# A two-layer attention and mixture-of-experts kernel: rank sums moved to TensorE, a softmax sum left out, one batch's residual adds moved to VectorE, and a denser queue of follow-up work

## The chip, the cores and the metric

The kernel runs on one core of one Trainium2 chip. Its time is the device time of one execution in microseconds, the median of several runs. A core has five instruction engines that matter here, each working through its own queue in order: TensorE (PE, with its weight loads shown apart as PEld), VectorE (DVE), ScalarE (ACT), GpSimd (POOL) and SyncE (SP), which here only starts transfers and reads registers. Data types are fp32 throughout.

## The reference

Two layers run on `x` of shape 8 x 512 x 256 (8 batches of 512 tokens, 256 channels). Each layer is an attention and a routed feed-forward, both behind a layer norm with a per-batch scale and shift, and both added back to `x` through a per-batch gate. Cut to what matters for the change:

```python
# layer 0 feed-forward, 4 experts, F = 1024
probs = softmax(xf @ router_w + router_b)
top_p, top_i = top_k(probs, 2)
top_p = top_p / sum(top_p)
out = sum over the two experts of top_p * (silu(xf @ w1[e]) * (xf @ w3[e])) @ w2[e]

# layer 1 attention; scores are 16 x 16 blocks, heads of width HD = 4
qkvw = x @ w_qkvw
o = softmax(q @ k.T * HD ** -0.5) @ v
x = x + ga * ((o * w) @ w_out)

# layer 1 feed-forward, 8 experts
route = sigmoid(x @ Wr + br)
out = max(route) * gelu(x @ W1[e]) @ W2[e]      # e = argmax(route)
```

The gates of layer 0's two experts are divided by their own sum. A common factor on both, such as the softmax's denominator, cancels there. Layer 0's attention is a running sum over tokens (a causal one), so it needs a scan over the 512 tokens of a batch for every head.

## The kernel before

**Chunks.** A feed-forward is not computed for all experts and all tokens. Tokens are sorted by expert into slots in DRAM (`hs`), and TensorE works on tiles of 128 rows of one expert. Six `Moe` objects hold six chunks: `m0` and `m1` are layer 0, four batches each (35 tiles each, two experts per token); `m2` and `m3` are layer 1 for the even batches, `m4` and `m5` for the odd ones (two batches each; 13 tiles each are run in the main order).

**A route.** `route(i)` is a generator that puts batch `i` of a chunk into slots, in four parts that a `yield` separates. Part one normalises `x` (`stats`, `normed`; bn_stats is L180). Part two transposes (`ptr`, L506), computes the logits (`pl`, L511), and transposes the modulated rows back (`prow`, L519) into `ht`, the rows to be scattered. Part three adds the bias (`z`, L527), takes the layer's function, and finds the chosen expert with `first_max` (L455 to L460), which leaves a one-hot `ch` for each token and choice. For layer 0, `now` is the sum of both choices (L546). Still in part three, VectorE writes `pre` (L560 to L566): `pre[:, t]` holds how often each expert was chosen by the tokens of earlier groups of 128, started from the running count of earlier batches. The fourth part, after a `yield`, ranks each token among those of its expert: `pk` is `tri` (a triangle of ones) times `now` (L569), plus `ones` times `pre` (L570). After another `yield`, VectorE makes slot numbers of the ranks (`rank`, `at`, `pos`, L573 to L582), and GpSimd starts one scatter per group and choice (`indirect_dma_start`, L586). `table()` then multiplies `ones` by the running count (`pn`, L603), and makes with some twenty small VectorE operations the table from which SP reads each tile's expert and first row.

**Layer 0's attention.** `attend0(b)` runs scans on VectorE (L411) and products on TensorE (`pv` L405, `poa` L422). Its results go to `residual` (L233, L234): VectorE multiplies by the gate, GpSimd adds to `x`. Batches 0 to 3 run before `m0`, woven with the routes of `m0`: batch `b`'s attention goes beside the route of batch `b - 1`, and the route of batch 3 (`HB - 1`, `HB` is 4) stands alone, followed by `m0.table()`. Batches 4 to 7 and the routes of `m1` go beside the tiles of `m0`.

**The order of tiles and steps.** `Line.run(m, steps, n, at, follow)` writes the tiles of a chunk in program order. A tile is a first half of the up-products (`up`, L760), the second half of the tile before's down-products (`down`, L775), the load of the next tile's rows (`xs`, transposed at L733), and then its own second halves. Twice in each tile, `n(j) / 2` steps are taken from the generator `steps`. So `n` is the number of steps beside a tile, and `at` names work for certain tiles (negative keys count from the end; `until(m4, steps)` takes steps until `m4` has its table). There is no planner: each engine does its instructions in the order in which the program wrote them.

**Layer 1's attention.** `attend(half, ...)` is such a generator: `half` 0 is batches 0 to 3 beside `m1`, `half` 1 is batches 4 to 7 beside `m2`, `m3` and `m4`. It goes in 16 units (4 output chunks of 4 units each). `step(u, v, w)` writes one unit's VectorE operations (a product, four sums, a maximum, reductions; L1011 to L1065), and every operation is followed by a `yield`; a full unit is 16 of them. GpSimd has part of the products (`far`, L996, and `farv`, L1031). `project` writes the projections (`pqk`, L978). When all four units of a chunk are done, `finish(i, after)` is put at the end of a list `behind`. `finish` transposes `o` (`pot`, L1078), copies it with ScalarE (`owT`, L1083), multiplies by the output weights (`pao`, L953), adds to `x` on VectorE (L957), and then runs what `then` holds for this chunk: for `half` 1 the routes of `m4` (chunks 0 and 1), with `m4`'s table, and of `m5` (chunks 2 and 3), with `m5`'s table. `beside(main)` passes on the steps of a unit and, after every third one, takes one step from the first generator in `behind`. Whatever is left of `behind` is taken after the last unit.

After a chunk is computed, `fetch_results` loads its rows back (`yl`, GpSimd's queue, L810), and `combine` multiplies by the gate and adds to `x` (L825 and L829).

```python
a2 = chain(attend(0, owA), m2.route(0), m2.route(1), ready(m2))
line.run(m1, a2, lambda j: 11.5 if j > 2 else 0, {...}, m2)
steps = attend(1, {}, {0: [m4.route(0)], 1: [m4.route(1), ready(m4)], 2: ..., 3: ...})
line.run(m2, steps, lambda j: 11 if j > 5 else 0, {..., 11: [until(m3, after)]}, m3, J=m2.J - 2)
line.run(m3, steps, lambda j: 11, {-3: [until(m4, steps)]}, m4, J=m3.J - 2)
line.run(m4, steps, lambda j: 6, {-3: [until(m5, steps)]}, m5, J=m4.J - 2)
drain(steps)
line.run(m5, iter(()), lambda j: 0, {...}, J=m5.J - 2)
```

Of the kernel before, what the change touches and what calls it, by code (L numbers as in the profile page):

```python
# [9 lines left out]
F32 = mybir.dt.float32  # L10
# [4 lines left out]
P = 128  # L15
# [13 lines left out]
def kernel(  # L29
# [200 lines left out]
    def residual(po, gate, b, t, name):  # L230

        tmp = wk.tile([P, D], F32, tag="tmp", name=name, bufs=2)
        nc.vector.tensor_mul(tmp, po, gate)  # L233
        nc.gpsimd.tensor_tensor(x[b][:, t, :], x[b][:, t, :], tmp, ALU.add)  # L234

# [226 lines left out]
    class Moe:  # L462
# [19 lines left out]
        def route(self, i):  # L482
# [51 lines left out]
            if l == 0:  # L534
                s = wk.tile([P, NT], F32, tag="rs", name=f"s{b}")
                nc.vector.tensor_reduce(s, z, AX.X, ALU.max)
                nc.vector.tensor_tensor(z, z, bcast(s, E), ALU.subtract)
                nc.scalar.activation(z, z, AF.Exp)
                nc.vector.tensor_reduce(s, z, AX.X, ALU.add)
                nc.vector.reciprocal(s, s)  # L540
                nc.vector.tensor_mul(z, z, bcast(s, E))
                first_max(z, E, m[0], ch[0], f"a{b}")
# [15 lines left out]

            pre = fp.tile([P, NT + 1, E], F32, tag=f"pre{E}", name=f"pre{bm}", bufs=3)
            if i == 0:  # L560
                nc.vector.memset(pre[:, 0], 0.0)
            else:
                nc.vector.tensor_copy(pre[:, 0], self.run_)
            for t in range(NT):
                nc.vector.tensor_add(pre[:, t + 1], pre[:, t], now[:, t])
            self.run_ = pre[:, NT]  # L566
            yield
            pk = ps_m([P, NT, E], f"pk{bm}")
            nc.tensor.matmul(pk, tri, now, start=True, stop=False)  # L569
            nc.tensor.matmul(pk, ones, pre[:, :NT], start=False, stop=True)  # L570
            yield
# [387 lines left out]
    def attend(half, owTs, then={}):  # L959
# [138 lines left out]
        def beside(main):  # L1098
            for n, _ in enumerate(main):
                yield  # L1100
                if n % 3 == 2 and behind:
                    if next(behind[0], behind) is behind:
                        behind.pop(0)
# [71 lines left out]
    def late():  # L1175
# [10 lines left out]
    after = late()  # L1186
    line.run(m2, steps, lambda j: 11 if j > 5 else 0, {
        0: [fetch_all(m1)],
# [7 lines left out]
    }, m3, J=m2.J - 2)  # L1196
    line.run(m3, steps, lambda j: 11, {-3: [until(m4, steps)]}, m4, J=m3.J - 2)
    line.run(m4, steps, lambda j: 6, {-3: [until(m5, steps)]}, m5, J=m4.J - 2)
    drain(steps)
# [75 lines left out]
```

## Time and profile before

Three runs took 1987.05, 1991.45 and 2002.29 us. The profiled execution took 2008.8 us by the same measure, 0.9% over their median; in it 2007.1 us lie between the first and the last instruction.

| | |
|---|---|
| median of the runs | 1991.45 us |
| profiled execution, its span | 2008.8 us, 2007.1 us |
| TensorE busy | 1764.3 us, 88% |
| VectorE busy | 1259.4 us, 63% |
| ScalarE, GpSimd busy | 717.4 us, 589.8 us |
| transfers | 488.6 MB, 243 GB/s |
| mean granted TensorE clock | 0.932 |

The span falls into stages, by the first and last products of each chunk in the trace: first attention and routing to about 330 us; `m0` to 880; `m1` to 1380; `m2` to 1567; `m3` to 1749; `m4` to 1888; `m5` to 1987; then the last results. The shares of busy time are means over stages of different kinds, and say little by themselves.

The costliest lines show what fills TensorE:

```profile
L760 PE MATMUL p<-xT,w 128*128 128x128 f32 x6144 | 770.2, 282 | 29.3 <-DMA w<-in_W_dram 17.9
L775 PE MATMUL po<-w_d,g 128*128 128x256 f32 x1952 | 483.3, 388 | 33.1 <-DVE g L767 22.8
L234 POOL TENSOR_TENSOR x<-x,ra 128x256 f32<-128x256 f32 x32 | 24.8, 780 | 141.2 <-DVE ra L233 141.0
L565 DVE TENSOR_TENSOR pre<-pre,ch 128x8 f32<-128x8 f32 x32 | 6.4, 202 | 0.4
L570 PE MATMUL pk<-pre,ones 128*128 128x16 f32 (+1 forms) x32 | 7.2, 307 | 5.2 <-DVE pre L565 5.2
```

Each row has the line, the engine and operation, the tile written and the tiles read, the shape, the count, then busy us and mean ns of one, then the idle time of the engine just before these instructions and what ended most of it. The up- and down-products are 71% of TensorE's busy time. The rows that the change touches are small: 24.8 us on GpSimd for all residual adds, 6.4 us on VectorE for layer 1's sums of `pre`, 7.2 us on TensorE for their products.

### The profile page before, as it was taken

To read this page: it belongs to the slowest core of one execution; us is meant where nothing else is said; L and a number is where in the kernel's file an instruction comes from. 1 tells how busy PE (TensorE), PEld (TensorE's weight loads), DVE (VectorE), ACT (ScalarE), POOL (GpSimd) and SP (SyncE) were. 2 spreads that over 40 slices of the span, in tenths; PEclk is the share of its full clock that TensorE was granted. 3 is DMA by queue.
4 is the path that set the end of the run, shared out by engine and by line. 5 is a ranking of instruction groups with operands and counts; after the bars stand their busy time and mean duration, and the time that the engine had idled before them with its cause. 6 is when DMAs were issued, how large, how long until landed. Compare 5 with 4: busy or idle time off the path is not lost.

```text
span 2007.1 us, 32461 instructions
## 1 busy us (share of the span) xinstructions
PE 1764.3 (88%) x11336; PEld 1541.1 (77%) x11336; DVE 1259.4 (63%) x2228; ACT 717.4 (36%) x1372; POOL 589.8 (29%) x564
## 2 busy tenths in 40 slices
PE   6786866989989989989999999998969989799895
PEld 3354436878878878879899898897868878788785
DVE  5786875443443532225999999722599999986200
ACT  5053112321312212216444435532545546355221
POOL 1033132121121121222444533123245464542110
PEclk8797887999999999989999999999989999899898
DMA  7877768899899997886786777888744655579795
GB/s 231 214 221 198 173 170 277 234 310 279 255 289 280 295 312 237 289 312 231 229 277 229 230 236 230 269 284 295 260 138 135 216 176 185 187 246 344 248 348 167
DMA packets 328536, 488.60 MB, mean 243 GB/s; under 512 B 24017, under 2 KB 184049, under 8 KB 327729
## 3 DMA queue, kind: packets, MB, share of 16 engines
q1 hardware_dynamic: 313840, 445.17, 71.9%
q0 software_dynamic: 14528, 41.31, 5.5%
q8 instruction: 92, 1.51, 0.3%
q14 instruction: 76, 0.61, 0.1%
HBM read 446.40 MB, written 45.27 MB: 245 GB/s over the span
## 4 chain that ended last, share of the span: by engine, by line
PE 53%; DVE 24%; DMA 9%; issue 7%; ACT 4%; POOL 2%; SPq 1%; another core or an unknown queue 1%; DVEq 0%; ACTq 0%; POOLq 0%
PE p L760 23%; PE po L775 13%; PE poa L422 3%; PE pv L405 3%; DVE u L411 3%; DMA w<-in_W_dram 3%; PE pqk L978 3%; DVE s L1019 2%; DVE o L1043 2%; DVE g L767 2%; DMA w<-in_w_dram 1%; DVE o L1060 1%; PE pl L511 1%; DVE u L414 1%; DMA ratio<-rows 1%
## 5 line engine op out<-in xcount | busy, mean ns | idle before, releaser
L760 PE MATMUL p<-xT,w 128*128 128x128 f32 x6144 | 770.2, 282 | 29.3 <-DMA w<-in_W_dram 17.9
L760 PEld LDWEIGHTS p<-xT,w 128*128 128x128 f32 x6144 | 750.3, 198 | 43.9 <-issue 18.0
L775 PE MATMUL po<-w_d,g 128*128 128x256 f32 x1952 | 483.3, 388 | 33.1 <-DVE g L767 22.8
L775 PEld LDWEIGHTS po<-w_d,g 128*128 128x128 f32 x1952 | 357.8, 194 | 87.5 <-DVE g L767 27.9
L790 POOL DMA_INDIRECT ys<-y,to x122 | 151.4, 1241 | 676.8 <-ACT xT L735 413.1
L765 ACT ACTIVATE g<-p 128x512 f32<-128x512 f32 x244 | 145.7, 597 | 482.4 <-PE p L760 411.9
L767 DVE TENSOR_TENSOR g<-g,p 128x512 f32<-128x512 f32 x140 | 95.6, 683 | 293.8 <-PE p L760 238.7
L411 DVE TENSOR_TENSOR_SCAN u<-ratio,pv 128x512 f32<-128x512 f32 x128 | 149.6, 1204 | 54.7 <-PE pv L405 35.5
L405 PE MATMUL pv<-hT,wv_sb 128*128 128x512 f32 x256 | 138.8, 664 | 34.4 <-DVE u L411 27.4
L996 POOL TENSOR_TENSOR far<-q 128x1024 f32<-128x1024 f32 x64 | 133.0, 2079 | 115.8 <-DVE pr L1054 75.7
L422 PE MATMUL poa<-wo_sb,hd 128*128 128x256 f32 x512 | 129.1, 401 | 18.6 <-DVE hd L416 18.3
L782 ACT ACTIVATE y<-po,xs 128x256 f32<-128x256 f32 x122 | 57.7, 473 | 234.4 <-PE po L775 188.1
L422 PEld LDWEIGHTS poa<-wo_sb,hd 128*128 128x128 f32 x512 | 98.7, 199 | 53.6 <-DVE hd L416 32.8
L586 POOL DMA_INDIRECT hs<-ht,pos x96 | 110.2, 1148 | 94.6 <-DVE at L579 32.7
L978 PE MATMUL pqk<-wq_sb,hTa 128*128 128x128 f32 x1024 | 124.2, 280 | 5.3 <-ACT q L985 4.9
L978 PEld LDWEIGHTS pqk<-wq_sb,hTa 128*128 128x128 f32 x1024 | 121.5, 196 | 7.2 <-ACT q L985 5.4
L1031 POOL TENSOR_TENSOR farv<-s,q 128x1024 f32<-128x1024 f32 x32 | 81.6, 2550 | 102.4 <-DVE pr L1028 84.5
L405 PEld LDWEIGHTS pv<-hT,wv_sb 128*128 128x128 f32 x256 | 48.1, 206 | 75.6 <-DVE u L411 34.6
L825 DVE TENSOR_TENSOR yl<-yl,gb 128x512 f32<-128x512 f32 (+1 forms) x24 | 20.6, 865 | 130.9 <-DMA yl<-ys 130.9
L1019 DVE TENSOR_TENSOR s<-s,far 128x1024 f32<-128x1024 f32 x64 | 89.3, 1398 | 0.7 <-POOL far L996 0.7
L414 DVE TENSOR_TENSOR u<-u,factor 128x1024 f32<-128x1024 f32 x64 | 78.1, 1220 | 1.6 <-issue 0.2
L1028 DVE TENSOR_TENSOR pr<-s,q 128x1024 f32<-128x1024 f32 x64 | 77.6, 1215 | 0.1
(205 smaller groups left out, 2003.7 us busy)
## 6 DMA issues: line engine op xcount, KB each, us to landing
w<-in_w_dram SPq DMA_DIRECT2D x280, 512.0 KB
w_d<-in_w_dram SPq DMA_DIRECT2D x140, 512.0 KB
w<-in_W_dram SPq DMA_DIRECT2D x104, 512.0 KB
w_d<-in_W_dram SPq DMA_DIRECT2D x104, 512.0 KB
ratio<-rows SPq DMA_DIRECT2D x128, 256.0 KB
factor<-rows SPq DMA_DIRECT2D x128, 256.0 KB
xs<-hs SPq DMA_DIRECT2D x122, 129.0 KB
yl<-ys POOLq DMA_DIRECT2D x32, 256.0 KB
```

The lines of the kernel that those rows point to most:

```text
L405: nc.tensor.matmul(pv, wv_sb[:, k, j * P : (j + 1) * P], hTs[b][:, k, :], start=(k == 0), stop=(k == KD - 1),)
L411: nc.vector.tensor_tensor_scan(out=u[:, i], data0=w[0][:, i], data1=pv, initial=0.0, op0=ALU.mult, op1=ALU.add)
L422: nc.tensor.matmul(po, hds[j][:, t * P : (t + 1) * P], wo_sb[:, j, :], start=(j == 0), stop=(j == NJ - 1),)
L586: ins = nc.gpsimd.indirect_dma_start(out=self.hs, out_offset=bass.IndirectOffsetOnAxis(ap=pos[c][:, t : t + 1], axis=0), in_=ht[c][:, t, : ...
L760: nc.tensor.matmul(p1[:, f * P : (f + 1) * P], ws[n][:, k, f * P : (f + 1) * P], u["xT"][:, k, :], start=(k == 0), stop=(k == KD - 1),)
L765: nc.scalar.activation(gq, pp[0], AF.Silu if l == 0 else AF.Gelu)
L767: nc.vector.tensor_mul(gq, gq, pp[1])
L775: nc.tensor.matmul(u["po"], u["g"][:, q * NF // 2 + f, :], u["w2"][q][:, f, :], start=(q == 0 and f == 0), stop=(q == 1 and f == NF // 2 - 1),
L790: ins = nc.gpsimd.indirect_dma_start(out=self.ys, out_offset=bass.IndirectOffsetOnAxis(ap=to, axis=0), in_=y, in_offset=None,).ins
L978: nc.tensor.matmul(pq[:, hh], hT[:, k, hb * 4 + hh].rearrange("p b r -> p (b r)"), wq_sb[:, k, i, gh].rearrange("p d w g -> p (d w g)"), s ...
L996: ins = nc.gpsimd.tensor_tensor(t, part(u, 0, d, True), part(u, 1, d, False), ALU.mult).ins
L1019: nc.vector.tensor_add(s, s, far[u, d])
```

## The change

Five edits:

1. In `residual`, the add to `x` of batch 3 goes to VectorE; those of the other batches stay on GpSimd.
2. In a layer-0 route, the sum of the exponentials, its reciprocal and the multiplication by it are left out. The chosen gates are still divided by their own sum.
3. `pre` is gone. `pk` is now `tri` times `now`, plus for t = 1 to 3 `ones` times `now` shifted by t groups, plus (in a second or later batch of the chunk) `ones` times the running count of the batches before, read as a broadcast. The running count `run_` is a new tile of its own: a reduction of `now` over its groups on VectorE, written after the matmuls, and an add of the count before. The `yield` stands ahead of all this now, so no VectorE sum is left between `now` and the `yield`.
4. `beside` takes a step of `behind` after every second step, not every third.
5. Beside `m2` and `m3` 10.5 steps are taken in a tile, not 11, and beside `m4` 7, not 6.

```diff
@@ residual
-        nc.gpsimd.tensor_tensor(x[b][:, t, :], x[b][:, t, :], tmp, ALU.add)
+        (nc.vector if b == HB - 1 else nc.gpsimd).tensor_tensor(x[b][:, t, :], x[b][:, t, :], tmp, ALU.add)
@@ Moe.route, l == 0
                 nc.scalar.activation(z, z, AF.Exp)
-                nc.vector.tensor_reduce(s, z, AX.X, ALU.add)
-                nc.vector.reciprocal(s, s)
-                nc.vector.tensor_mul(z, z, bcast(s, E))
@@ Moe.route
-            pre = fp.tile([P, NT + 1, E], F32, tag=f"pre{E}", name=f"pre{bm}", bufs=3)
-            if i == 0:
-                nc.vector.memset(pre[:, 0], 0.0)
-            else:
-                nc.vector.tensor_copy(pre[:, 0], self.run_)
-            for t in range(NT):
-                nc.vector.tensor_add(pre[:, t + 1], pre[:, t], now[:, t])
-            self.run_ = pre[:, NT]
             yield
+            before_, self.run_ = self.run_, fp.tile([P, E], F32, tag=f"run{E}", name=f"run{bm}", bufs=2)
             pk = ps_m([P, NT, E], f"pk{bm}")
             nc.tensor.matmul(pk, tri, now, start=True, stop=False)
-            nc.tensor.matmul(pk, ones, pre[:, :NT], start=False, stop=True)
+            for t in range(1, NT):
+                nc.tensor.matmul(pk[:, t:], ones, now[:, : NT - t], start=False, stop=i == 0 and t == NT - 1)
+            if i:
+                nc.tensor.matmul(
+                    pk, ones, before_.unsqueeze(1).to_broadcast([P, NT, E]), start=False, stop=True
+                )
+            nc.vector.tensor_reduce(self.run_, now.rearrange("p t e -> p e t"), AX.X, ALU.add)
+            if i:
+                nc.vector.tensor_add(self.run_, self.run_, before_)
             yield
@@ attend, beside
-                if n % 3 == 2 and behind:
+                if n % 2 and behind:
@@ the main order
-    line.run(m2, steps, lambda j: 11 if j > 5 else 0, {
+    line.run(m2, steps, lambda j: 10.5 if j > 5 else 0, {
...
-    line.run(m3, steps, lambda j: 11, {-3: [until(m4, steps)]}, m4, J=m3.J - 2)
-    line.run(m4, steps, lambda j: 6, {-3: [until(m5, steps)]}, m5, J=m4.J - 2)
+    line.run(m3, steps, lambda j: 10.5, {-3: [until(m4, steps)]}, m4, J=m3.J - 2)
+    line.run(m4, steps, lambda j: 7, {-3: [until(m5, steps)]}, m5, J=m4.J - 2)
```

## The prediction, made before the changed kernel had run

> **What bounds the kernel now.** I read the page's slices first, then the windows by stage, then the waits of TensorE and VectorE, then the timelines round the three places that the change touches.
>
> ```profile
> PE   6786866989989989989999999998969989799895
> DVE  5786875443443532225999999722599999986200
> PEclk8797887999999999989999999999989999899898
> ...
> 1100.00:1200.00 100.00, 96.57 (x738) 91.89 (x737) 100.00 (x100) 38.62 (x72) 44.22 (x20) 1.00 0.72 234
> 1500.00:1600.00 100.00, 89.10 (x619) 82.46 (x620) 95.10 (x158) 50.52 (x89) 44.87 (x31) 0.92 0.55 174
> 1600.00:1700.00 100.00, 90.19 (x617) 83.39 (x616) 96.42 (x119) 57.42 (x98) 56.30 (x33) 0.95 0.53 175
> 1700.00:1800.00 100.00, 83.19 (x531) 75.54 (x530) 94.58 (x144) 48.63 (x89) 41.97 (x30) 0.90 0.64 206
> 1889.00:1987.00 98.00, 93.55 (x622) 84.43 (x621) 4.81 (x4) 27.11 (x61) 14.26 (x15) 1.00 0.88 301
> ```
>
> A digit of the first three rows is a slice of 50 us. In a window row stand the length, then busy us of PE, PEld, DVE, ACT and POOL, the clock, the DMA share and GB/s. The reader is to see four regimes. Up to 330 us (first attention, batches 0 to 3) no engine is full and the clock is low: a chain through VectorE sets the pace. From 330 to about 1380 (m0, m1) TensorE is 93 to 98% busy at nearly full clock: TensorE bounds, and in m1 VectorE is full beside it. From about 1446 to 1831, where attention 1 runs beside m2, m3 and m4, VectorE is 95% busy while TensorE is at 83 to 90% and loses clock: VectorE bounds. After 1889 (m5) TensorE is alone.
>
> ```profile
> PE pk L569 <- DVE ch L460: 17.1, 4, 9.0
> PE pk L569 <- DVE now L546: 8.3, 2, 7.2
> PE pk L570 <- DVE pre L565: 5.2, 2, 3.0
> ```
>
> These are TensorE's waits (us, times, longest) inside a route. The first two are for the chosen expert, before any rank is summed; only the third is for the sum that the change takes away.
>
> ```profile
> 269.41 1.03 POOL L498 TENSOR_SCALAR ht<-slot 128x1 f32<-128x1 f32 x4 [7.33 <-DMA hs<-ht,pos]
> 270.52 1.41 POOL L234 TENSOR_TENSOR x<-x,ra 128x256 f32<-128x256 f32 x2
> ...
> 271.28 0.43 DVE L180 BATCH_NORM_STATS2 stf<-x 128x6 f32<-128x256 f32 x1 [4.51 <-POOL x L234]
> ...
> 1828.20 1.23 DVE L825 TENSOR_TENSOR yl<-yl,gb 128x1024 f32<-128x1024 f32 x1 [5.62 <-DMA yl<-ys]
> ...
> 1831.55 0.60 PE L1078 MATMUL pot<-ident,o 128*64 128x128 f32 x4 [0.87 <-DVE o L1065]
> ...
> 1845.20 1.03 PE L953 MATMUL pao<-wg,owT 128*128 128x256 f32 x4
> ...
> 1880.89 5.25 PE L760 MATMUL p<-xT,w 128*128 128x128 f32 x32 [2.43 <-DMA w<-in_W_dram]
> ```
>
> In timeline lines the bracket is the idle time before and what ended it. At 269 GpSimd stands in its queue before an instruction that waits for a scatter's DMA, and batch 3's residual adds behind it come 4.5 us late. At 1831 the last attention value is there, but the last output product pao comes at 1845.2, and m5's first products at 1880.9.
>
> **A. Batch 3's residual on VectorE, the softmax's sum.** ra is ready at 265.92 to 266.8. Four adds leave GpSimd (780 ns each) and go to VectorE; no trace row has that line there, the nearest is x<-x,pao L957 of the same shape: 414 ns, so 4 x 0.41 = 1.7 us added. They take away VectorE's idle 4.51 and the 0.61 us at 277.89: -5.1. The chain from here (statistics, transposes, logits, choice, rank, table, xs load) ends in m0's first product at 327.50, so nearly all of it arrives: -3.4 us. GpSimd only gets work off its queue; its L498 still waits for the scatter, but only its small columns of ht depend on it. The softmax's sum is three VectorE operations in the chain, 149 + 170 + 175 ns, start to start 298.12 to 298.72: -0.6 on route 3. In routes 0 to 2 the same three operations and some of the rank adds shorten work beside which TensorE waits 0.3 to 3.9 us (pv <- s L539 3.9): of the some 3.4 us removed I take -1.0. Routes of m1 lie under TensorE-bound m0: nothing, VectorE waits there for TensorE (g L767 <- p L760, 238.7 us), and if that cover went each route would cost or give some 1.3 us.
>
> **B. The rank by TensorE.** Per route VectorE loses a memset or copy (166 ns) and four adds (159 or 202 ns: 0.77 us in a row at 1858.77), and gets a reduction (near 0.17, as L455) and one add: -0.5 us on route 3, where the adds at 302.86 stand between now and the second matmul. TensorE loses one matmul of a route and gets 3, or 4 in a second or later route: over 16 routes (8 layer-0, 8 layer-1, 6 chunks) 16 of pk<-pre become 48 + 10 = 58, so +42. Each fp32 matmul is two records. The nearest row, pl (same stationary form, 4 columns), takes 0.112 us from record to record at full clock and 0.22 at half: 0.23 us a matmul, 9.4 us in all. The Trainium skill, "TensorE: Matmul & The Clock Gate", section "Back-to-back issue gap", puts small matmuls on an issue floor of about 25 ns, which for 84 records would make 2.1 us; but its stationary load is P/1.2 (section "LDWEIGHTS"), 107 ns for 128 columns, and here each record brings its own load. The row decides. By place: 11 in 0 to 330, of which the four or so of route 3 lie on the chain at half clock (the clock is 0.5 from 296.7 to 330.8): +1.2; 11 beside m0, TensorE-bound, without cover: +2.4; 5 beside m1: +1.1; the other 15 beside m2 to m4 in TensorE's 13% idle: 0, or 3.4 if that idle closes. Against this stands the wait for pre in layer 1, 2.99 at 1536.55 and 2.20 later; the tri matmul stays where it was, so the waits for ch stay. After the 2.99 us the clock is halved for 6.8 us (p x32 takes 5.68 us at 1538.6, 3.57 at full clock), so up to 2 us more. Because VectorE bounds there I count -1.3.
>
> Part A sums with B's share of it to -3.4 - 0.6 - 1.0 - 0.5 + 1.2 = -4.3 us (ends -1 and -8: the wait moves to ACT's normalisation, or all of it arrives). The TensorE-bound part is +3.5 (0.9 by the issue floor, 5 if halved clock falls on it).
>
> **C. Denser queue, quotas.** The queue behind a chunk (transposes of o, output products, residuals, route, table) now advances on every second step of the main generator, 8 times in a unit of 16, not 5. Counting generator steps, m4's table comes at step 192, not 206, of 301 in all; the end of m2 is at 81, not 85; of m3 at 221, not 236; the loop of m4 gives the remainder at 7 a tile, so attention ends in m4's tile 9 or 10 either way. Moved with these steps: 4 transposes and 4 ACT copies per pot, 8 matmuls, 4 adds on VectorE per output, per route 4 GpSimd columns, one pl group, four scatters, and the table; SP's order (xs and weight loads) hardly moves; ACT has five table loads (1283 ns) fewer in its order. VectorE's total hardly changes, and 15 steps of some 1.25 us only go from m2 and m3 to m4: in a stretch where it is full, 0. What I count is on the end chain. Before, pots and outputs of the last chunk are interleaved with tile products: 1831.55 to 1846.2, 14.7 us. After, the same four pots and four outputs stand almost without tile work between, which by their own durations is some 7.5: -7 (ends 0 and -9: ACT's copies between). yl's load on GpSimd stood behind four scatters at 1810.8 to 1816.4; it comes before them in the new order, so VectorE's idle 5.62 at 1828.20 shrinks by some -2.6 (0 to -5.6). Small VectorE operations of six layer-1 routes, 0.25 each: -1.5. New: a route's logits come sooner behind the residual, so VectorE may stand at z <- pl (37.7 us over all now, 15 times): +2.4 taken (0 to 10). Sum -8.7, with B's -1.3 -10.
>
> Sum: -4.3 + 3.5 - 10.0 = -10.8, some -11 us. The profiled execution lasted 2008.8 us (span 2007.1), 0.9% over the median of the runs shown, 1991.45. A difference carries over: 1998 against 2008.8, 1981 against 1991.45.
>
> **Rivals.** *Nothing arrives (1991).* In m2 to m4 VectorE has 27.2 us idle in 396; moving steps in a full engine gives nothing, and the loads of m5's weights and rows (2.99 and 2.43 us before 1877.8 and 1880.9) take up the end chain's gain. Then A and B remain, -4.3 + 3.5 - 1.3 = -2.1: 1989; with A half, 1991. For it: windows 95%; against: 14.7 us of pot to output, with nothing on VectorE in 1838.3 to 1841.2.
>
> *Slower: two queues in step (2008).* TensorE in m3 has about 12.2 us of work in a tile of 14 us, VectorE at 10.5 steps 13.1. The denser queue puts pot, pao, x, z one or two steps behind their producers, in order on both engines. As soon as such a wait is longer than the slack of 0.9 us a tile, VectorE idles, and TensorE, waiting for o in turn, drops to half clock: the half-clock pieces in this trace are 3.4 to 10.2 us long. The Trainium skill, on the same page, section "HAM oscillation — how this bites in real kernels", says idle gaps past some 3.4 us do it; here the gap of 2.99 has the clock at 0.5 from 1535.7 to 1542.5, and by the rule that stall would have cost 3 us and not 5. 16 such pairs (4 chunks of 4 pots) at 1.3 us with the -11 lost and +3.5 kept make some +17 to +25: 2008 to 2016. It decides if the added idle passes 11 us. For it: x <- pao 12.9 us in 11 waits already; against: finish still leaves two steps before its transposes except in the last chunk.
>
> *More arrives (1963).* TensorE is idle for 68.6 us over 1380 to 1900, at a clock of 0.90 to 0.95. If the new order also closes a quarter of that idle time, 17 us go on top of the -11. Against it: VectorE is as full there as it can be.
>
> *The change doesn't do what it says*: tri still waits for ch, 17.1 us; only 5.2 us of pk's waits go. That is already in the sum.
>
> **How the numbers follow.** Forecast 0.45 (own range 1974 to 1988), nothing 0.22 (1987 to 1996), slower 0.20 (1996 to 2016), more 0.13 (1960 to 1974). 1% is about what a measurement of this kernel tells from no change, since its three runs span 0.8%; its bounds are 1971.5 and 2011.4. Faster by over 1%: all but a little of more, 0.12, and a tenth of the forecast, 0.05: 0.17. Slower by over 1%: half of the slower case, 0.10, and 0.01. Same: 0.72. The range leaves out a tenth at each end: 1968 to 2005.
>
> **What would show it.** A: no idle before stf near 271, m0's first product 4 to 5 us before 327.5; wrong if it stays within 1 us. B: pk<-now with 6 to 8 records per route, wait <- pre gone, m0 two us longer from first to last product. C: pot to last pao under 9 us, no yl wait over 3.5 us, m5's first products some 11 us nearer to m1's end than now (about 500 us). The forecast is wrong if VectorE's idle in 1446 to 1842 grows above 40 us, or if the stage from m2's start to m5's is not shorter.

## The result, and the profile after

The changed kernel took 2013.78 us (four runs, 2012.18 to 2024.6) beside 1989.82 us before: a ratio of 1.0129, with an interval of 1.0094 to 1.0165. It is 24 us slower, where 11 us of gain were forecast, and lies outside the range of 1968 to 2005.

The profiled execution of the changed kernel is a typical one: 2010.8 us of span, 2012.58 us by the measure of the runs. The profile shown of before (2007.1 us) was not. The kernel before was therefore profiled a second time: 1987.4 us of span, 1989.1 us by the measure of the runs. This second profile stands for "before" from here on. The first has lost 18 us beside the second between 306 and 823 us, in m0, where the transfer engines are busy for 0.9 of the time.

First, the windows of the changed kernel (columns as in the prediction: length, busy us of PE, PEld, DVE, ACT and POOL, clock, DMA share, GB/s):

```profile
1500.00:1600.00 100.00, 86.66 (x577) 78.24 (x576) 94.28 (x138) 54.24 (x94) 57.59 (x34) 0.92 0.61 193
1600.00:1700.00 100.00, 94.96 (x644) 88.10 (x642) 94.89 (x121) 50.66 (x92) 50.35 (x30) 0.92 0.56 178
1700.00:1800.00 100.00, 83.57 (x540) 76.03 (x540) 97.37 (x141) 47.17 (x86) 50.67 (x32) 0.91 0.71 232
1889.00:1987.00 98.00, 93.51 (x629) 84.98 (x628) 4.90 (x4) 28.00 (x64) 14.91 (x15) 1.00 0.88 300
```

By these rows little has happened: VectorE is as full as it was, TensorE as idle. The waits tell more (us in all, times, longest). TensorE and VectorE of the changed kernel:

```profile
PE pk L560 <- DVE ch L460: 20.2, 7, 9.0
...
PE pxs L732 <- DMA xs<-hs: 11.4, 4, 6.9
...
PE pd L366 <- POOL before L363: 10.2, 3, 9.5
...
PE pxs L732 <- DVE skip L632: 7.3, 1, 7.3
...
DVE x L956 <- PE pao L952: 36.7, 7, 32.3
...
DVE stf L180 <- POOL x L234: 19.7, 25, 0.8
```

The same waits in the second profile of before:

```profile
PE pxs L733 <- DMA xs<-hs: 6.5, 5, 2.4
...
PE pd L366 <- POOL before L363: 3.8, 2, 3.4
...
DVE x L957 <- PE pao L953: 11.0, 12, 2.9
```

New are one wait of 9.5 us for GpSimd at 318 us, two of about 7 us before the first rows of a chunk (pxs; the profile names what came last, in one the rows' transfer, in the other VectorE), and one of VectorE for TensorE of 32.3 us. That last one is the end of attention 1, here in the timelines of VectorE and TensorE of the changed kernel:

```profile
1812.76 1.23 DVE L828 TENSOR_TENSOR yl<-x,yl 128x1024 f32<-128x1024 f32 x1
1846.28 0.42 DVE L956 TENSOR_TENSOR x<-x,pao 128x256 f32<-128x256 f32 x1 [32.29 <-PE pao L952]
...
1838.59 1.89 PE L774 MATMUL po<-w_d,g 128*128 128x256 f32 x8
1840.32 1.04 PE L1077 MATMUL pot<-ident,o 128*64 128x128 f32 x8
...
1845.08 3.75 PE L952 MATMUL pao<-wg,owT 128*128 128x256 f32 x16 [0.42 <-ACT owT L1082]
```

and the same place in the second profile of before:

```profile
1812.08 0.58 DVE L1065 TENSOR_TENSOR o<-o,q 128x256 f32<-128x256 f32 x1
...
1812.81 0.60 PE L1078 MATMUL pot<-ident,o 128*64 128x128 f32 x4 [1.97 <-DVE o L1065]
...
1824.83 1.03 PE L953 MATMUL pao<-wg,owT 128*128 128x256 f32 x4
```

Before, TensorE waits 1.97 us for the last attention value: VectorE sets the end. After, VectorE has that value at 1807.0, 5.7 us earlier than before, and TensorE comes to it at 1840.3, out of tile products, without a wait. VectorE's way did become shorter, from 386.1 to 373.5 us (first score to last value of attention 1). It bought nothing, because TensorE had become the bound in m4.

Where the time went can be read by stages. ScalarE copies every finished tile out (y, 122 times); a stage ends with the copy of a chunk's last tile. In us:

```
                  to m0's end     m1    m2 and m3     m4    m5 and rest    span
before, first        880.1      500.7     368.7     138.9      118.7     2007.1
before, second       866.4      497.2     366.8     138.6      118.4     1987.4
changed              874.5      496.9     367.6     152.4      119.4     2010.8
```

Two places lose: everything up to m0's end, 8.1 us, and m4, 13.8 us. In m2 and m3 together nothing is lost, in spite of the stalls before the rows: VectorE sets the pace there.

TensorE's time splits into idle time, busy time at a granted clock of 0.50, and busy time at full clock. `after_again` is a second profile of the changed kernel:

```
                  span      idle    busy at 0.50    busy at 1.00
before, second   1987.4    231.8       164.7           1590.9
changed          2010.8    240.0       182.0           1588.8
after_again      2008.4    243.7       168.5           1596.2
```

A busy us at 0.50 is counted as half a us of work (sixteen products take 3.79 us at half clock and 1.95 at full, shown below). Then the 23.4 us of the changed kernel are 8.2 of idle time, 8.7 of slower clock and 6.5 of added work; the 21.0 us of after_again are 11.9, 1.9 and 7.2. The added work is alike in both; how the rest falls on idle time and clock is not.

### The profile page after: what moved, and what is told of

Same layout as the page of the kernel before. It is cut to its first block, busy times and chain, and to the rows that moved or that the text cites. A ratio compares the mean times of both kernels' runs of the same rounds, so it can differ in the third digit from the quotient of the medians.

```text
span 2010.8 us, 32574 instructions
## 1 busy us (share of the span) xinstructions
PE 1770.8 (88%) x11420; PEld 1551.4 (77%) x11420; DVE 1240.6 (62%) x2154; ACT 710.6 (35%) x1367; POOL 606.1 (30%) x560
## 4 chain that ended last, share of the span: by engine, by line
PE 55%; DVE 26%; issue 6%; DMA 6%; ACT 5%; POOL 1%; SPq 1%; DVEq 0%; ACTq 0%; POOLq 0%
PE p L759 23%; PE po L774 13%; PE pv L405 4%; PE poa L422 4%; DVE u L411 3%; DVE s L1018 3%; PE pqk L977 3%; DVE o L1042 2%; DMA w<-in_W_dram 2%; DVE o L1059 2%; DVE g L766 1%; PE pl L511 1%; PE pao L952 1%; DVE s L1048 1%; DVE sum L1044 1%
## 5 line engine op out<-in xcount | busy, mean ns | idle before, releaser
L774 PE MATMUL po<-w_d,g 128*128 128x256 f32 x1952 | 476.3, 384 | 23.7 <-DVE g L766 16.2
L789 POOL DMA_INDIRECT ys<-y,to x122 | 156.0, 1279 | 630.5 <-ACT xT L734 422.1
L422 PE MATMUL poa<-wo_sb,hd 128*128 128x256 f32 x512 | 128.5, 399 | 19.7 <-DVE hd L416 19.3
L585 POOL DMA_INDIRECT hs<-ht,pos x96 | 116.4, 1213 | 95.0 <-issue 30.9
```

The lines of the kernel that those rows point to most:

```text
L422: nc.tensor.matmul(po, hds[j][:, t * P : (t + 1) * P], wo_sb[:, j, :], start=(j == 0), stop=(j == NJ - 1),)
L585: ins = nc.gpsimd.indirect_dma_start(out=self.hs, out_offset=bass.IndirectOffsetOnAxis(ap=pos[c][:, t : t + 1], axis=0), in_=ht[c][:, t, : ...
L774: nc.tensor.matmul(u["po"], u["g"][:, q * NF // 2 + f, :], u["w2"][q][:, f, :], start=(q == 0 and f == 0), stop=(q == 1 and f == NF // 2 - 1),
L789: ins = nc.gpsimd.indirect_dma_start(out=self.ys, out_offset=bass.IndirectOffsetOnAxis(ap=to, axis=0), in_=y, in_offset=None,).ins
```

## The experiments

Ratios are to the kernel before on the same chip, with 95% intervals.

### What the profile of before is worth

`b_again` is the kernel before without an edit.

> The kernel before, profiled once more. The profile shown of it spans 2007 us, while its runs without a profile have a median of 1990; the changed kernel's profile spans 2011 against 2014. Theory 1 (the profiled execution of before was a slow one): this profile spans about 1988, and the stages from m2's start to m4's end are some 10 to 20 us shorter than in the first profile. Theory 2 (a profile costs this kernel time): it spans about 2007 again. In both the ratio is 1.000.

Measured: 0.9994 [0.9976, 1.0012], span 1987.4 us. Theory 1 held, but the place was wrong: the first profile lost its time in m0, not between m2 and m4. A single profile of this kernel can be 18 us off in one stage, so small differences in the end time are read from ratios. The later stages are steadier: the two profiles of before differ by 3.5 us in m1, 1.9 in m2 and m3, 0.3 in m4.

### The parts alone

`route_parts` has the edits of a route (1, 2 and 3), `rank_only` edit 3 alone, `queue_quota` edits 4 and 5, `quota_only` edit 5, `queue_only` edit 4:

```diff
 queue_only, queue_quota
-                if n % 3 == 2 and behind:
+                if n % 2 and behind:
 quota_only, queue_quota
-    line.run(m4, steps, lambda j: 6, ...
+    line.run(m4, steps, lambda j: 7, ...
...
```

> Before with the three edits of a route alone: residual of batch 3 on VectorE, no softmax sum, rank by TensorE; queue and quotas as before. Theory 1 (the loss lies in the order of the queue and the quotas): 1988 to 1992, ratio 0.998 to 1.001, with m0's first product 2 to 4 us earlier and m0 2 us longer. Theory 2 (the 42 matmuls that no idle time covers make the loss): 2000 to 2014, ratio 1.006 to 1.012.

Measured: 1.0072 [1.0050, 1.0094], as theory 2.

> Before with the denser queue and the three quotas alone, routes as before. Theory 1: 2010 to 2020, ratio 1.010 to 1.016; VectorE done with attention 10 to 25 us ahead of the last transposes of o on TensorE, and TensorE idle some 7 us before m3's first rows and before m4's. Theory 2: 1985 to 1995.

Measured: 1.0090 [1.0060, 1.0119], the stalls before the first rows of m3 and m4 5.8 and 8.0 us, VectorE done at 1800.8 and the last transposes at 1839.7.

> Before with the rank by TensorE alone. Theory 1: 1990 to 1994, ratio 1.000 to 1.003 (42 matmuls of 0.23 us, a third of them uncovered, less the waits for the sum). Theory 2: 2000 to 2014, ratio over 1.005.

Measured: 1.0083 [1.0052, 1.0113]. So neither theory alone: the order and the rank each lose, about alike. The longest new wait of rank_only on TensorE is at batch 3's route, the second of m4:

```profile
1696.14 1.11 PE L519 MATMUL prow<-ident,hTr 128*128 128x128 f32 x4
1710.27 0.64 PE L562 MATMUL pk<-ch,tri 128*128 128x32 f32 x2 [13.01 <-DVE ch L460]
1710.72 1.43 PE L564 MATMUL pk<-ch,ones 128*128 128x24 f32 x6
```

In before some products of the tile stood between the row transposes and the rank, and TensorE waited 4.45 us for the choice and 2.20 for pre. Here they stand ahead of the transposes, and TensorE waits 13.0 us, in a stretch of 30.7 us at a clock of 0.50. But this wait is not where the time went: m2 and m3 together took 367.8 us, beside 366.8. And `extra_mm` below, which sums the rank as before, waits 10.8 and 3.0 us at the same place, with 366.1 us for m2 and m3. What rank_only loses in its profile lies before m0's end (9.2 us) and in m4 (7.3 us).

> Before with the three quotas alone. By TensorE's order the projection falls behind m3's first rows, and stays ahead of m4's. Theory Q: a stall of 5 to 7 us before m3's first rows, none at m4's; 1996 to 2002, ratio 1.003 to 1.006. Rival R: 1990 to 1994.

Measured: 0.9994 [0.9979, 1.0008]. TensorE did stall for 5.95 us before m3's first rows, and for 10.3 us at a rank near 1696, and no time was lost: m2 and m3 together took 363.4 us, and VectorE set the pace. Theory Q fell for this kernel.

> Before with the denser queue alone. By TensorE's order the projection stays ahead of m3's first rows, and half of the next one falls behind m4's. Theory Q: no stall at m3's first rows, one of 2 to 4 us at m4's; 1991 to 1997, ratio 1.000 to 1.003. Rival D (the denser queue itself makes TensorE and VectorE wait for each other): 2000 to 2008, with x <- pao and z <- pl each up by 5 us or more.

Measured: 1.0046 [1.0028, 1.0064], no stall above 1.9 us before m3's or m4's first rows, and the last transposes one tile later, at 1824.6. Half a point lost by the density alone: between the two theories' sizes. Of the waits that rival D named, x <- pao grew by 8.1 us (11.0 to 19.1, 12.5 of it once, at the end of attention 1), z <- pl by 2.3 only. TensorE's stall of 10.5 us at a route's first transposes (1582) is its largest new one, and m2 and m3 are no longer for it (366.1 us); m4 is, by 8.8 us.

### The swap on GpSimd

The GpSimd timeline of the changed kernel at the start of m0:

```profile
317.56 0.23 POOL L361 COPY before<-tr 128x32 f32<-128x32 f32 x1
317.87 0.25 POOL L363 TENSOR_TENSOR before<-before,tr 128x32 f32<-128x32 f32 x1
323.53 1.03 POOL L498 TENSOR_SCALAR ht<-slot 128x1 f32<-128x1 f32 x4 [5.41 <-DMA hs<-ht,pos]
324.64 0.25 POOL L363 TENSOR_TENSOR before<-before,tr 128x32 f32<-128x32 f32 x1
```

and of before (second profile):

```profile
319.61 0.22 POOL L361 COPY before<-tr 128x32 f32<-128x32 f32 x1
319.91 0.58 POOL L363 TENSOR_TENSOR before<-before,tr 128x32 f32<-128x32 f32 x2
325.47 1.03 POOL L498 TENSOR_SCALAR ht<-slot 128x1 f32<-128x1 f32 x4 [4.99 <-DMA hs<-ht,pos]
```

The small columns of batch 4's second rows (L498) wait for a scatter to land. In the changed kernel they stand ahead of the last add of batch 5's running sums, which TensorE needs. The text before the prediction says that each engine works in the order in which the program wrote its instructions. That is wrong. The two adds of L363 come from one loop with nothing between them, and in the changed kernel L498 runs between the two. So the build puts each engine's instructions in an order of its own, and an edit elsewhere can move them: no line of these two was edited.

`after_pool` puts that one group back by an ordering without a wait:

```diff
+            sums[b] = (the last add of `before` of batch b)
...
+                    if l == 0 and c and b == HB:
+                        tc.add_manual_dep(ins, sums[b + 1].name, BEHIND, reason="behind the sums")
```

> The changed kernel with one GpSimd instruction group put back: the small columns of batch 4's second rows (L498, which wait for a scatter of batch 3 to land) stand behind the last add of the running sums of batch 5, as in before, and not ahead of it. All else keeps its place. Theory P (this swap costs TensorE 5.4 us at 318 us, and m0 begins that much later): 2007 to 2010, 4 to 6 us under the changed kernel (2013.8), the wait pd <- before falls from 9.5 to some 4 us, m0's first product comes 5 us earlier. Rival (the wait is absorbed by m0's first weights, which then come no earlier): 2012 to 2015, with a wait for w in its place.

Measured: 1.0096 [1.0066, 1.0126]; the median, 2015.96, is to be set against 1995.88 of before on that chip, not against 2013.8. TensorE's timeline of after_pool, at the wait that was 9.46 us:

```profile
318.05 0.74 PE L366 MATMUL pd<-before,ones 128*128 128x96 f32 x2 [3.03 <-POOL before L363]
```

m0's first product comes at 327.3, beside 333.1 in the changed kernel and 329.5 in after_again, which has the wait of 9.45 us too. A head start of 2 to 6 us is shown. At m0's end it cannot be seen any more: 871.1 us, beside 874.5 and 871.0. Nor in the end time: 1.0096 beside 1.0129 and 1.0080 of the changed kernel's two measurements. `soft_pool` (edits 1 and 2 with this hold) and `route_pool` (edits 1 to 3 with it) ask the same from the other side.

> Before with part A alone (batch 3's residual adds on VectorE, no softmax sum), and with GpSimd's group of small columns held behind batch 5's sums, as it stood in before. Theory P: m0's first product 3 to 5 us earlier than in the kernel before, and all after it as before: ratio 0.997 to 0.999. Rival (m0's stream of weights takes the head start back): 0.9995 to 1.001 with the first product as early.

Measured: 0.9982 [0.9969, 0.9995], as theory P. m0's first product comes 7.0 us earlier (322.8, not 329.8), at m0's end 1.5 us of it are left. TensorE waits 9.4 us for weights on that way, 6.4 before, which is some of what is taken back. This version beats both kernels, 1988.6 us beside 1992.4 of before.

> Before with the three edits of a route, and GpSimd's group held behind batch 5's sums. Without that hold the ratio was 1.0072. Theory P (5.4 us of it are the swap on GpSimd): 1.0045. Rival (absorbed): 1.007.

Measured: 1.0057 [1.0038, 1.0075] beside 1.0072 without the hold. The intervals overlap; the sign fits theory P, the size is open.

### The price of a small matmul

`extra_mm` leaves the rank as it was and adds the changed kernel's 42 matmuls on a tile of zeros; `extra_mm3` adds 126. What is computed does not change.

```diff
-            nc.tensor.matmul(pk, ones, pre[:, :NT], start=False, stop=True)
+            nc.tensor.matmul(pk, ones, pre[:, :NT], start=False, stop=False)
+            for n in range(3 if i else 2):
+                nc.tensor.matmul(pk, ones, none_[:, :, :E], start=False, stop=n == (2 if i else 1))
```

> Before, with the sum for the rank still made by VectorE and the 42 matmuls of the changed kernel added beside it, on a tile of zeros: 2 more in a chunk's first route, 3 in the others. TensorE's and GpSimd's other instructions keep their places but for single ones. Theory M (the price is that of the matmuls, 42 x 0.23 = 9.4 us, of which the third in TensorE-bound stages counts, and halved clock): 1.5 to 5 us, ratio 1.001 to 1.0025. Rival N (the rest of the loss of rank alone, 0.8%, is in these matmuls too): ratio 1.006 or more.

Measured: 1.0076 [1.0046, 1.0105], 15 us, the size of rival N, with a wide spread (1997.36 to 2014.51). The profile is of the shortest of the five executions and shows 8.3 us more than the second one of before: 7.0 before m0's end and 0.5 in m4. Where the others lose more is not shown.

> Before with the VectorE sum kept and three times as many matmuls added as the changed kernel adds: 126 on a tile of zeros, 6 in a chunk's first route and 9 in the others. The 42 gave 1.0076 [1.0046, 1.0105]. Theory F (TensorE has no free time on its path in any stage: each costs its full 0.23 us): 126 x 0.23 = 29 us, ratio 1.013 to 1.016. Theory T (only those of the TensorE-bound stages count, a third to a half): 9 to 15 us, 1.005 to 1.008. Theory H (they cost more than themselves, by halved clock): 1.02 or more.

Measured: 1.0168 [1.0139, 1.0197], 33.6 us for 126: 0.27 us each. Three rank groups in the trace give the time of the matmuls themselves (lines of TensorE's timeline of extra_mm3, 12 and 18 records, two records a matmul):

```profile
443.52 1.49 PE L574 MATMUL pk<-none__106,ones 128*128 128x16 f32 x12
...
1321.21 1.50 PE L574 MATMUL pk<-none__106,ones 128*128 128x32 f32 x12
...
1332.82 2.17 PE L574 MATMUL pk<-none__106,ones 128*128 128x32 f32 x18
```

2.17 us for 9 matmuls is 0.24 us each, at full clock. By the end time theory F holds, each at its full price. By stages it does not (the times in the trace hold those at half clock too):

```
 extra_mm3, us                     to m0's end     m1 to m3      m4
added matmuls                          66             45         15
their time on TensorE in the trace    20.0           15.1        5.5
stages longer than before by          30.7            0.7        3.7
```

The 45 beside m1, m2 and m3 took 15.1 us of TensorE and made these stages 0.7 us longer, less than two profiles of before differ there: they were covered. The 66 before m0's end cost half as much again as their own time; in m0 TensorE also idles 26.4 us, beside 19.3 before, and why is not shown. The 22 of extra_mm there took 7.4 us and cost 7.0. That the average of all 126 comes near their own time is luck. The division is theory T's, the price higher than T gave. It is read from one profile; its execution was the shortest of five, 2.5 us under their median.

### Cover before a chunk's first rows

In TensorE's order before, the projections pqk of the next unit stand between a chunk's last table and the first rows of the next chunk, and fill the way from table to rows. The changed quotas and queue leave them behind those rows. `after_old_quota` has the old quotas; `after_cover` takes steps just before the rows:

```diff
 after_cover
         11: [until(m3, after)],
+        12: [some(steps, 4)],
...
-    line.run(m3, steps, lambda j: 10.5, {-3: [until(m4, steps)]}, m4, J=m3.J - 2)
+    line.run(m3, steps, lambda j: 10.5, {-3: [until(m4, steps)], -1: [some(steps, 8)]}, m4, J=m3.J - 2)
```

> The changed kernel with the quotas of before (11, 11, 6), denser queue and routes as changed. In TensorE's order most of the projection that the changed kernel has behind the first rows of m3 stands ahead of them again, and half of that at m4. Theory Q (the quotas took away the work that covers the way from table to first rows): the stalls of 7.3 us before m3's first rows and 6.9 us before m4's fall under 3 us each, 2000 to 2006. Rival R (VectorE sets the pace there, and the stalls only move): 2010 to 2015, with other stalls of the same sum.

Measured: 1.0085 [1.0054, 1.0116], 2012.4 us, as rival R. The stalls before the rows fell to 1.95 and 1.3 us, and one of 13.3 us at a route's first transposes came in their place.

> The changed kernel with 4 more steps of attention taken just before m3's first rows are read, and 8 before m4's: both projections stand ahead of those rows in TensorE's order again, and the transposes of the last chunk in m4's tile 9 as in before, not in tile 10. Theory Q (the projections cover the way from table to rows): the stalls of 7.3 and 6.9 us fall under 2.5 us each, ratio to before 1.003 to 1.008, where the changed kernel has 1.0129. Rival R (the stalls move to another wait of the same size): 1.011 or more.

Measured: 1.0095 [1.0071, 1.0120]. TensorE's timeline, first of the changed kernel, then of after_cover:

```profile
1545.30 0.66 PE L732 MATMUL pxs<-ident,xs 128*128 128x128 f32 x2 [7.28 <-DVE skip L632]
...
1723.52 0.66 PE L732 MATMUL pxs<-ident,xs 128*128 128x128 f32 x2 [6.92 <-DMA xs<-hs]
```

```profile
1546.67 0.41 PE L732 MATMUL pxs<-ident,xs 128*128 128x128 f32 x2 [1.77 <-DMA xs<-hs]
...
1595.02 2.17 PE L506 MATMUL ptr<-ident,ht 128*128 128x128 f32 x8 [13.50 <-ACT ht L205]
```

The ratio lies between the two theories' ranges. The stalls before the rows went, as theory Q said, and a stall of 13.5 us at a route's first transposes stands in their place, with 23.9 us at half clock round it. Of the mechanism rival R is right: TensorE runs into the next thing that it is ahead of. m2 and m3 together took 367.6 us with the stalls before the rows and 369.8 without.

### The dense queue beside m4

In the changed kernel nothing stands in TensorE's order between the row transposes of batch 5's route and its rank. Its timeline there:

```profile
1783.15 1.95 PE L759 MATMUL p<-xT,w 128*128 128x128 f32 x16
...
1794.25 1.95 PE L519 MATMUL prow<-ident,hTr 128*128 128x128 f32 x8
1802.79 0.61 PE L560 MATMUL pk<-ch,tri 128*128 128x32 f32 x2 [6.59 <-DVE ch L460]
1803.20 1.43 PE L562 MATMUL pk<-ch,ones 128*128 128x24 f32 x6
...
1805.61 3.79 PE L759 MATMUL p<-xT,w 128*128 128x128 f32 x16 [0.46 <-ACT xT L734]
```

Sixteen products take 3.79 us after the stall, where 1.95 is their time at full clock. The clock is at 0.50 for 17.1 us here, from 1792.8. `after_sparse4` goes back to every third step in attention 1's last four units only, and `after_again` is the changed kernel on the same chip.

```diff
-                if n % 2 and behind:
+                if (n % 3 == 2 if sparse else n % 2) and behind:
```

> The changed kernel, with the queue advanced on every third step again, not every second, beside the last quarter of attention 1 (the units of chunk 3, which run beside m4). In TensorE's order nothing stands between the row transposes of batch 5's route and the rank in the changed kernel; here twelve products of a tile and more do. Theory S (the denser queue writes dependent steps with too little work between): the wait pk <- ch of 6.6 us near 1803 and the 20 us of halved clock round it go; 4 to 10 us under the changed kernel, ratio 1.008 to 1.011. Rival D (VectorE's or the rows' way sets m5's start): within 3 us of the changed kernel.

> The changed kernel once more, on the chip of these runs, so that the kernels made from it can be set against it: ratio 1.010 to 1.0145; its profile again with the stalls of some 7 us before m3's and m4's first rows and of 6.6 us at pk <- ch in m4 (theories Q and S), or, if those were chance, without them.

Measured: after_sparse4 1.0060 [1.0045, 1.0074], 2004.5 us; after_again 1.0080 [1.0051, 1.0109], 2010.5 us, each below the range expected of it. TensorE's timeline of after_sparse4 at the same place:

```profile
1792.59 1.08 PE L519 MATMUL prow<-ident,hTr 128*128 128x128 f32 x8
...
1796.88 2.05 PE L759 MATMUL p<-xT,w 128*128 128x128 f32 x16
...
1803.37 0.31 PE L560 MATMUL pk<-ch,tri 128*128 128x32 f32 x2
```

and the window of these 60 us, first of after_again, then of after_sparse4:

```profile
1780.00:1840.00 60.00, 49.89 (x311) 44.86 (x312) 27.41 (x43) 21.95 (x48) 18.77 (x17) 0.86 0.87 285
```

```profile
1780.00:1840.00 60.00, 54.95 (x365) 48.53 (x363) 33.72 (x64) 32.24 (x69) 17.91 (x17) 1.00 0.89 301
```

The wait at the rank is gone, the clock is full, and TensorE gets 365 matmul records done, not 311. m5's first products come at 1867.7, not 1879.7, and m4 takes 139.7 us, not 153.0, where before took 138.6. That is 12 us in the profiles and 6 us in the medians. The profile of after_sparse4 is of the shortest of its 21 executions (1996.68 us, median 2004.5), so it shows the gain too large. The intervals of the two ratios overlap; but four of the five executions of after_again took longer than 19 of those 21. The mechanism of theory S is shown, its size in the end time is near 6 us.

### Whether the parts add up

`after_pre_pool` is the changed kernel with edit 3 taken back and the hold on GpSimd.

> The changed kernel with the rank's sum back on VectorE (no added matmuls), and GpSimd's group behind batch 5's sums. If the parts add up (A and hold 0.9982, queue and quotas 1.0090): 1.006 to 1.008. If the rank's matmuls cost nothing beside this queue (TensorE's stalls hide them): 1.010 or more.

Measured: 1.0078 [1.0053, 1.0103], as after_again, and in the range of parts that add up; the interval reaches the other range too. By ratios, the parts give -0.18% (edits 1 and 2 with the hold), +0.75 (edit 3: route_pool less soft_pool), some +0.15 (swap) and +0.90 (queue and quotas), 1.6% together; the changed kernel has 0.8 to 1.3. The stages show where they overlap (us longer than in the second profile of before, one profile each):

```
                 to m0's end    m1    m2 and m3     m4    m5 and rest    all
soft_pool           -1.5        2.4      0.5        0.6      -0.1        2.0
rank_only            9.2        1.8      0.9        7.3      -0.2       19.1
route_pool           6.4        2.7      1.3       10.4       0.1       21.1
queue_quota          1.5       -0.1      3.7       16.3       0.1       21.7
changed              8.1       -0.3      0.7       13.8       1.0       23.4
after_again          4.6       -0.8      0.9       14.4       1.7       21.0
after_pre_pool       0.3        2.3      5.5       13.4      -0.9       20.7
after_sparse4        5.3       -0.7      0.9        1.1       0.8        7.5
```

Before m0's end it is edit 3 that loses. Six profiles without it reach that point at 864.9 to 867.9 us (only the first one of before, at 880.1, is late), nine with it at 871.0 to 875.6, and extra_mm at 873.4. In m4 the rank in one piece loses 6 to 10 us with the old queue (route_parts has 6.2), where extra_mm's five matmuls lose 0.5: so it is less their own time than their place in the order. Queue and quotas lose 16 there, the queue alone 8.8. Together they lose no more than queue and quotas alone, and with the sparse queue beside m4 nearly nothing.

## Why the prediction failed, step by step

The forecast by stages, and what two profiles of the changed kernel showed beside the second one of before, in us:

```
                  forecast    changed    after_again
start and m0        -1.9         8.1         4.6
m1                   1.1        -0.3        -0.8
m2, m3 and m4      -10.0        14.5        15.3
```

The step that failed is C's -10 us. It counted the denser queue on VectorE, +2.4 us (0 to 10) of wait for logits, and had no term for what the queue does to TensorE's order: "attention ends in m4's tile 9 or 10 either way". In its place the runs show a route on TensorE without work between its steps, and m4 13.8 us longer; after_sparse4 takes that to 1.1. A second step failed at the start: -4.3 us of head start and +2.4 us of matmuls in m0 came to +4.6 to +8.1.

**What bounds the kernel.** VectorE was read as the bound from 1446 to 1831, since it is 95% busy. For m2 and m3 that held before and after: 366.8 and 367.6 us, whatever TensorE stalled for. In m4 the margin was small: 1.97 us of wait at the last transposes of before. There TensorE became the bound. The prediction called moves in a full engine worth 0 and did not ask how far the second engine was.

**A.** Right in what it said of VectorE: no idle before stf (longest wait 0.8 us after, 4.5 in the profile that it read), and with edits 1 and 2 and GpSimd's order held the chain is 7.0 us shorter where 3.4 + 0.6 + 1.0 were counted. "Nearly all of it arrives" failed: 1.5 us are left at m0's end, 3.6 us (0.18%) in the end time. And "only its small columns of ht depend on it" failed for the changed kernel: an add that TensorE needs was ordered behind that group, and m0's first product came at 333.1 and 329.5 in two profiles, not 4 to 5 us before 329.8.

**B.** The price of a matmul from the row of pl (0.23 us) was right: 0.24 in the trace. The issue floor, 2.1 us for all, is out; the 107 ns for a load are near the 120 ns of a record. What was mis-sized is the time before m0's end: 1.2 + 2.4 us were counted for 22 matmuls, of the 11 at the start only four, and extra_mm loses 7.0 us there. The 0 for those beside m2 and m3 is borne out by extra_mm3, whose 45 beside m1 to m3 cost 0.7 us. In m4 the matmuls cost little (extra_mm 0.5 us), but the rank in one piece costs 7.3 us in rank_only, by its place in the order, which the prediction left out. The waits for pre went, as said (5.2 to 0).

**C.** The gain on the end chain came as forecast: pot to the last pao 8.5 us (1840.32 to 1848.8), not 13.0, and yl's wait of 5.8 us is gone. Its base failed: the pots come 27.5 us later. The transposes moved from tile 9 to tile 10 in TensorE's order, so VectorE's earlier end is spent waiting 32.3 us. The tile alone is not the loss, since after_sparse4 has them in tile 10 too. Beside m4 the denser queue leaves dependent steps of a route without work between, with 6.6 us of stall and 17.1 us at half clock. The sign that was named for a wrong forecast came true: VectorE idles 47.1 us in 1446 to 1842, over the 40, and from m1's end to m5's first products it takes 511 us, not less than 497.

**The rivals.** "Slower: two queues in step", 2008 to 2016 us at a chance of 0.20, was the nearest. Dependent steps too close, and half clock beside them, are what the runs show, but not where it said. It named pot, pao, x and z in four chunks; the runs show the rank in a route (by after_sparse4). And it expected VectorE to idle, while VectorE's idle within attention fell from 24.1 to 19.1 us. So that 2013.8 lies in its range is in part luck: its 16 pairs at 1.3 us were not there. "Against: finish still leaves two steps before its transposes" looked at the wrong pair of steps. Its half-clock pieces of "3.4 to 10.2 us" are those after 330 us; one of 34.1 us begins at 296.7.

What stays open: the share of the GpSimd swap in the end time, why extra_mm3's matmuls before m0's end cost more than their own time, and where the slower executions of extra_mm lose theirs. A kernel with all causes removed at once was not tried.

## What to carry to other kernels

When two engines are both near full, ask in each stage which one ends last and by how much: work taken from that one is worth only the margin to the other. Small matmuls "in idle time" were covered here where VectorE is full (m1 to m3) and cost their own time or more before m0's end, so price them by stage; an average over the kernel can come out right by luck. In an in-order queue count what stands between a step and the next step that depends on another engine's answer; an edit that makes a queue denser takes that work away. A long stall costs nothing where the other engine sets the pace: look at the length of the stage before giving it a price. Compare the built order of every engine, GpSimd's too, for instructions that no edit touched but that now wait behind something.

## What the runs showed of the hardware that was not expected

A VectorE copy of 4 integers took 0.15 us in before and 4.09 us in the changed kernel. The timeline of VectorE, and of GpSimd at that time:

```profile
1538.51 4.09 DVE L671 COPY otab<-tab 128x4 int32<-128x4 int32 x1
...
1538.34 2.36 POOL L1030 TENSOR_TENSOR farv<-s,q 128x1024 f32<-128x1024 f32 x1
1540.63 1.93 POOL L995 TENSOR_TENSOR far<-q 128x1024 f32<-128x1024 f32 x1
```

The copy starts 0.17 us after GpSimd's first product and ends with the second one, at 1542.6. It does so again at 1717.36 (3.81 us), and in after_again, after_sparse4 and after_pool twice, in after_cover once, each time within 0.05 us of the second product's end. In before, queue_quota and quota_only, where no product is running when the copy starts, it takes 0.15 us. The Trainium skill, "SBUF — State Buffer", section "SBUF: two separate sides", says that VectorE operations in a two-port mode and GpSimd take one pair of ports as an exclusive lock for a whole instruction; this fits, though the copy waited for two products and not one, and no run here took the lock away to prove it.

Half clock did not wait for a long stall. In the second profile of before the clock is at 0.50 for 6.8 us from 1517.6, with no wait of TensorE near it longer than 2.99 us (ended at 1518.06). In the changed kernel it falls to 0.50 at 1792.8, for 17.1 us, and the stall of 6.59 us begins only at 1796.2; before it stand a route's small products with pauses of 0.76 and 0.28 us.
